# A fused hybrid block on one core: PSUM pools in another order, routing weights as powers of e, row numbers and counts taken later

## The chip, the core and the metric

The kernel runs on one core of one Trainium2 chip. The metric is the device time of one launch in microseconds (us). A core has five engines that run their own instruction streams: TensorE (PE, with its weight loads as PEld), VectorE (DVE), ScalarE (ACT), GpSimd (POOL) and SyncE (SP, which here only issues DMAs). They meet at semaphores. Matmuls write to PSUM, which has eight banks[...].

## The reference

Two layers on an image batch `x` of 2 x 256 x 56 x 56. Layer 0 is a group norm, a 1x1 and a depthwise 3x3 convolution to q, k and v, neighbourhood attention (7x7 windows, one half of the heads with dilation 1, one with dilation 2) and a projection. Layer 1 turns the image into 6272 tokens of 256 channels and does linear attention and a mixture of experts:

```python
t = _to_tokens(x)
t = t + _L1_attn_ref(_ln_t(t), ...)          # linear attention, Q = elu(q)+1, K = elu(k)+1
t = t + _L1_ffn_ref(_ln_t(t), ...)           # 8 experts, the two best of each token
...
logits = xt @ Wr + br
probs = softmax(logits); top_p, top_idx = top_k(probs, 2)
weights = top_p / top_p.sum(axis=-1)         # of two: 1/(1+d) and d/(1+d), d = e^(m1-m0)
xn = layernorm(xt)
h = gelu(xn * ln_g[e] + ln_b[e]) @ W1[e] + b1[e]), y = h @ W2[e] + b2[e]
out = sum of weights * y of the two experts
```

## The kernel before

**Stages.** The convolutions of both images run beside the attention of image 0 (0 to some 420 us). Then the linear attention of the tokens of image 0 (`linear`, half 0) runs beside the rest of the convolutions, to 748 us; then the attention of image 1 (`Attention`, with the bank pool `Banks`) beside the first expert tiles, to some 1050 us; then the linear attention of image 1 (half 1) beside further expert tiles, to 1450 us; then the remaining expert tiles with the output. The 6272 tokens are taken in groups of four blocks of 128 rows (`order`), the last ones in smaller groups.

**Order.** Within `tc.manual_schedule` TensorE's order is the program's. The parts of a group are generators (`queries`, `message`, `feed_forward`, `route`), and strings such as "mqfpPPPPfmqfrfrff" say which one goes a step further: r is the route of the current group, p and P that of the group before it. The other engines' orders are set by a planner when the kernel is built, by priority and estimated readiness; `tc.issue_after(x)` puts an instruction behind x in that order. At run time each engine takes its instructions in its order.

**Routing (`route`).** A group's first step takes the router's logits (`pa`, evacuated to `la`), the token norm, and the normalised rows `row`. The second turns `la` back (L2058), finds the two best experts (`top_two`: maxima `ms`, one-hot `ohs`), adds up the counts per expert before each block (`before`, and the running `cnt`, L2066 to L2069) and computes the two weights of each token (`weights`, L2007: DVE subtracts, ACT does Exp at L2011, DVE the rest) into `row`. The third multiplies with a triangular matrix (L2073, L2074: `pp`) for each token's slot in its expert's list, and casts it to `si`; the stores of the tokens to `y2` are issued from ACT (L1974). Four more steps scatter the rows to `xs` by indirect DMAs from POOL (L2089, helper L167), eight for a full group.

**The seam.** `layer1` leaves the end of the last two groups' routes of half 0 to a generator `ending`, whose five steps are taken inside the attention of image 1, at the step numbers in `ENDING`: the last group but one's `pp`; its scatters and the last group's second step; the counts of full tiles (`full_tiles`: a matmul on `cnt`, L1387, then DVE's table) and the last group's `pp`; its scatters; the rest of the table. From step `LEAD` (22) on, the expert tiles run one step at each attention step: `Experts.fetch` of tile 0 loads `xr` from `xs` once all scatters of these tokens have landed. The attention turns `ld` tiles with TensorE (L759, into `x` banks) and evacuates them to `qT` and `kT` (ACT L768, L771, L777, L784; DVE L779). A chunk is a score matmul `s_ps` (L644), Exp on ACT (L648), a product with a table on DVE (L649), and a value matmul `po` (L658).

**PSUM.** Pools of half 0, in order: `ps_a` two banks, `ps_h` three, `ps_q` two. When they close, the attention opens `po` (two banks), `x` (two), `s_ps` (four), in the same place. `ps_h` holds the feed-forward's results, read last by DVE (L1958); `ps_q` the queries' and the turned messages.

**Expert tiles (`Experts.run`).** For each tile of 256 rows: `fetch` of the next one (from SP: `xr`, L1536, w1e, L1540, w2e, L1544; DVE: `eq`, L1550, L1553, L1554, row numbers `idi`, L1552, and the expert's scale `so`, `sv`), first matmuls `ph` (L1600) with Gelu on ACT (L1604), `turn` of the next tile (TensorE L1569, DVE `xe` L1572, POOL `yt`, L1582), second matmuls `py` (L1618), DVE `yt` (L1624) and a scatter with addition to `y2` (POOL, L167).

Of the kernel before, what the change touches and what calls it, by code (L numbers as in the profile page):

```python
# [13 lines left out]
F32 = mybir.dt.float32  # L14
AF = mybir.ActivationFunctionType
ALU = mybir.AluOpType
# [45 lines left out]
NFS, NHS = 48, 5  # L62
NFI = 14
LEAD = 22
ENDING = (4, 6, 13, 15, 20)
XW = C + 4


# [57 lines left out]
def hybrid_kernel(ctx: ExitStack, tc: tile.TileContext, a: dict, out: bass.AP):  # L126
# [5 lines left out]
    make_identity(nc, ident)  # L132
    mhalf = const.tile([P, 4], F32, name="mhalf")
    nc.vector.memset(mhalf, -0.5)


    td = dram.tile([B * T, C], F32, name="td")
# [461 lines left out]
    class Attention:  # L599
# [116 lines left out]
        def run(self):  # L716
# [126 lines left out]
            def band0(r):  # L843
                yield blocks(8 * r + 16)
                if banks is not None and r == 0:
                    for k in range(2):
                        turning.extend(prepare(k))
                        if k == 0:
                            self.ahead[0, 0] = self.fetch(0, 0)
                    ready[0] = 2  # L850
                yield from prepared(r + 1, 1)
                spare = self.spare if r == 0 else None
                v0 = (spare or vp).tile([TT, 4, P], F32, name="v0", bufs=1 if spare else 2)
                for c in range(4):
                    nc.sync.dma_start(
                        v0[:, c, :],
                        yimg[8 * r : 8 * r + 8, c * KC : (c + 1) * KC, 2 * C : 2 * C + P],
                    )
                if banks is not None and r == 0:
                    self.ahead[0, 1] = self.fetch(0, 1)  # L860
                    self.ahead[1, 0] = self.fetch(1, 0)
                i0, i1 = max(0, 8 * r - 3), min(HH, 8 * r + 11)
                ni = i1 - i0
                sums = [None]

                def chunk(hf, c):
                    j0, j1 = max(0, KC * c - 3), min(WW, KC * c + 17)
                    q = qT0[:, i0:i1, j0:j1]
                    got = []

                    def first():
                        got.append(self.scores(
                            TT, [(kT0[r][:, c].rearrange("p r c -> p (r c)"), q, 0)],
                            self.table(0, (r > 0) + (r == NG - 1), (c > 0) + (c == 3)), j1 - j0,
                        ))

                    def rest():
                        if c == 2 * hf:
                            po = self.ps_o.tile([P, 2, 512], F32, name="po")
                            sums[0] = po[:, :, : ni * 31].rearrange("p k (i j) -> p k i j", j=31)  # L880
                        h0 = (0, 25)[hf]
                        sub = sums[0][:, :, :, j0 - h0 : j1 - h0]
                        self.values(
                            TT, got[0], [(None, q, 0, v0[:, c, :], sub[:, 0], sub[:, 1])], c == 2 * hf
                        )

                    return first, rest

                def done(hf):
                    h0 = (0, 25)[hf]  # L890
                    for j, a0, a1 in ((r, i0, 8 * r + 4), (r + 1, 8 * r + 4, i1)):
                        o = 8 * j - 4
                        accumulate(
                            strip0(j)[:, :, a0 - o : a1 - o, h0 : h0 + 31], sums[0][:, :, a0 - i0 : a1 - i0, :]
                        )
                    if hf == 0:
                        return
                    for j in (r, r + 1) if r == NG - 1 else (r,):
                        a0, a1 = max(0, 8 * j - 4), min(HH, 8 * j + 4)
                        self.normalise(  # L900
                            strips0.pop(j)[:, :, a0 - 8 * j + 4 : a1 - 8 * j + 4, :].rearrange("p k r c -> p k (r c)"),
                            o0[:, a0:a1, :].rearrange("p r c -> p (r c)"), (a1 - a0) * WW,
                        )

                for hf in range(2):
                    for c in (2 * hf, 2 * hf + 1):
                        yield from step(*chunk(hf, c), (lambda hf=hf: done(hf)) if c % 2 else lambda: None)
# [439 lines left out]
    class Experts:  # L1347
# [179 lines left out]
        def fetch(self, t, nh, pools):  # L1527

            run = self.tk.run
            full = nh == 2 and t < NTA  # L1530
            tab, k = (self.tab_h, t) if nh == 1 else (self.tab_a, t) if full else (self.tab_b, t - NTA)
            x = SimpleNamespace(t=t, nh=nh, full=full)
            xr = x.xr = pools.xr()[:, :nh, :]
            e = self.value(tab.tab[0:1, 0, k : k + 1], E - 1)
            r = self.value(tab.tab[0:1, 1, k : k + 1], E * RG + (NDUM - 1) * ST)
            ins = nc.sync.dma_start(xr, xs[bass.ds(r, nh * P), :].rearrange("(p j) c -> p j c", j=nh))  # L1536
            if full:
                apart(ins.ins, [f"xfull{run}"], [f"xlate{run}", f"fill{run}"])
            x.w1 = self.w.tile([P, 2, FF], F32, name="w1e")
            nc.sync.dma_start(  # L1540
                x.w1, a["L1_ffn_W1"][bass.ds(e, 1)].rearrange("one (ct p) f -> p (one ct) f", p=P)
            )
            x.w2 = self.w.tile([P, NJ, C], F32, name="w2e")
            nc.sync.dma_start(  # L1544
                x.w2, a["L1_ffn_W2"][bass.ds(e, 1)].rearrange("one (j p) d -> p (one j) d", p=P)
            )
            x.e = e
            x.eq = self.small.tile([P, 2], F32, name="eq")
            eq = x.eq[:, :nh]
            nc.vector.tensor_scalar(eq, xr[:, :, C + 3], tab.etm[:, k : k + 1], None, ALU.is_equal)  # L1550
            x.idi = self.small.tile([P, 2], mybir.dt.int32, name="idi", bufs=4)
            nc.vector.tensor_copy(x.idi[:, :nh], xr[:, :, C])  # L1552
            nc.vector.tensor_tensor(eq, eq, xr[:, :, C + 2], ALU.mult)  # L1553
            nc.vector.tensor_tensor(eq, eq, xr[:, :, C + 1], ALU.add)  # L1554
            so = self.small.tile([P, 4 + NJ, E], F32, name="so")
            nc.vector.tensor_tensor(
                so, self.sel, tab.oh[:, k, :].unsqueeze(1).to_broadcast([P, 4 + NJ, E]), ALU.mult
            )
            x.sv = self.small.tile([P, 4 + NJ], F32, name="sv")
            nc.vector.tensor_reduce(x.sv, so, AX.X, ALU.add)  # L1560
            return x

        def turn(self, x, pools):
# [7 lines left out]
            for ct in range(2):  # L1571
                newest[0] = nc.vector.tensor_scalar(  # L1572
                    x.xe[:, ct, :], px[:, ct, :nh, :].rearrange("p j t -> p (j t)"),
                    x.sv[:, ct : ct + 1], x.sv[:, 2 + ct : 3 + ct], ALU.mult, ALU.add,
                ).ins
            b2 = pools.b2e()
            nc.sync.dma_start(
                b2, a["L1_ffn_b2"][bass.ds(x.e, 1)].rearrange("one d -> (one d)").partition_broadcast(P)
# [61 lines left out]
    def linear(ph, tk, half, behind=None):  # L1640
# [4 lines left out]
        def pool(name, bufs, **kw):  # L1645
            return ph.enter_context(
                tc.tile_pool(name=f"{name}{run}{half}", bufs=bufs, reuse_waits="tile", **kw)
            )
# [1 line left out]
        bufs = {"e": 1, "s": 3, "t": 1, "q": 1, "w": 1, "k": 2, "l": 2}  # L1650
        pools = {k: pool(f"p3{k}", bufs[k]) for k in ("e t q w k l s", "e s t q k w l")[half].split()}
        kp, sm, tp, wqp, wp, wk, lp = (pools[k] for k in "estqwkl")
        ps_a, ps_h, ps_q = pool("p3pa", 2, space=PSUM), pool("p3ph", 3, space=PSUM), pool("p3pq", 2, space=PSUM)
        ps_k = pool("p3pk", 1, space=PSUM) if half else None
        tk.place(half, tp, lp)

# [324 lines left out]
        def top_two(rt, lg, up, lb, scale, row, n):  # L1981
# [22 lines left out]
                ohs.append(oh)  # L2004
            return ohs, ms

        def weights(rt, ms, row, n):  # L2007

            r = rt.sm.tile([P, 4], F32, name="rsum")[:, :n]
            nc.vector.tensor_tensor(ms[1], ms[1], ms[0], ALU.subtract)  # L2010
            nc.scalar.activation(ms[1], ms[1], AF.Exp)  # L2011
            nc.vector.tensor_scalar(r, ms[1], 1.0, None, ALU.add)
            nc.vector.reciprocal(r, r)
            nc.vector.tensor_tensor(row[:, :n, C + 1], ms[1], r, ALU.mult)
            nc.vector.tensor_scalar(ms[0], ms[1], -1.0, 1.0, ALU.mult, ALU.add)
            nc.vector.tensor_tensor(row[:, :n, C + 2], ms[0], r, ALU.mult)

        def route(n0, n, lb):
# [48 lines left out]
            for k in range(n):  # L2067
                nxt = before[:, k + 1, :] if k < n - 1 else cnt
                nc.vector.tensor_tensor(nxt, before[:, k, :], m[:, k, :], ALU.add)  # L2069
            weights(rt, ms, row, n)  # L2070
            yield
            pp = ns.bank()[:, : 4 * E].rearrange("p (k e) -> p k e", e=E)
            nc.tensor.matmul(pp[:, :n], rt.tri, m[:, :n], start=True, stop=False)  # L2073
# [9 lines left out]
            store(n0, n)  # L2083
            late = [f"xlate{run}"] if (n0, n) in order[early1:] else []
            yield
            for k in range(n):
                with tc.issue_after(newest[1]) if late else nullcontext():
                    for kk in range(K):
# [75 lines left out]
    def layer1(whole, tk, conv_ctx=None, conv=None, behind=None):  # L2164


        run = tk.run
        conv = conv or none

        def fill(n=1):  # L2170
            for _ in range(n):
# [263 lines left out]
```

## Time and profile before

| | us |
|---|---|
| Median of 3 runs | 2003.97 (2000.4 to 2013.45) |
| The profiled execution | 2003.56, of it span from first to last instruction 2001.8 |
| Granted TensorE clock, mean | 0.969 |
| Linear attention, half 0, ends (last `pa`) | 748.2 |
| First L759 of image 1's attention | 751.0 |
| First scores of image 1 | 762.0 |
| First expert matmul (L1600) | 798.0 |
| First matmul of half 1's keys | 1048.8 |
| Last `py` | 1978.4 |

A line of the order of time has: start, duration, engine, line, operation, out<-in, shapes, count, and in brackets the engine's idle time before it and what ended that wait. A line of the waits has: engine, what it waited to do, on what, the sum in us, how often, the longest. Copies of engine names with a q (SPq, ACTq) are sequencers: they wait, branch and issue.

| Operation (before) | engine | number | mean us |
|---|---|---|---|
| Exp of routing weights L2011, 128x4 | ACT | 14, four with a table load of 1.28 | 0.20 |
| power of -1/2, L2043, 128x4 | POOL | 14 | 1.0 |
| power of -1/2, L261, mostly 128x2 | POOL | 90 | 0.70 to 0.80 |
| row scatter to `xs`, L167 | POOL | 98 | 1.03 |
| row numbers L1552 | DVE | 53 | 0.18 |

### The profile page before, as it was taken

The page shows a single profiled execution, that of the slowest core. Times are in us where ns is not written, and L with a number is a line of the kernel's source. Part 1 is how long each engine was busy: PE and PEld are TensorE (multiplying, and loading weights), DVE is VectorE, ACT ScalarE, POOL GpSimd, SP SyncE. Part 2 cuts the span into 40 slices and gives each one's busy share as a digit, 9 for nine tenths or more (in the row PEclk, how much of TensorE's full clock was granted, in tenths as well). Part 3 has the DMA queues.
Part 4 walks back from the last instruction along what each step waited for, and adds up shares of the span by engine and source line. Part 5 has one row for each costly group of instructions (what it writes and reads, how often), then busy time and mean ns, then how long its engine had stood idle before and what let it go on. Part 6 is the DMA issues. An engine that isn't in the chain of part 4 may idle for free.

```text
span 2001.8 us, 27731 instructions
## 1 busy us (share of the span) xinstructions
PE 1842.0 (92%) x9996; PEld 1308.3 (65%) x9996; DVE 1094.2 (55%) x2733; ACT 704.5 (35%) x1331; POOL 582.2 (29%) x634
## 2 busy tenths in 40 slices
PE   6999898988889996899989989999899999999996
PEld 3545354556555654566668756567688888888885
DVE  6978988888887746555557434554531212121221
ACT  2333324324434323445536433323322232323332
POOL 4630221025102444111126311445422222222221
PEclk9999999989999996999999999999999999999998
DMA  4753432340001534654474211114577676766995
GB/s 112 160 138 110 133 92 75 111 146 17 25 38 42 157 85 145 193 152 134 129 201 127 56 34 37 48 57 132 156 230 200 188 199 189 198 190 195 299 279 161
DMA packets 200153, 268.85 MB, mean 134 GB/s; under 512 B 30953, under 2 KB 158615, under 8 KB 199761
## 3 DMA queue, kind: packets, MB, share of 16 engines
q1 hardware_dynamic: 167920, 223.95, 37.0%
q0 software_dynamic: 19728, 27.54, 7.5%
q10 hardware_dynamic: 12352, 15.43, 2.2%
q8 instruction: 83, 1.36, 0.3%
q14 instruction: 70, 0.57, 0.1%
HBM read 200.19 MB, written 70.95 MB: 135 GB/s over the span
## 4 chain that ended last, share of the span: by engine, by line
PE 47%; DMA 4%; DVE 4%; ACT 3%; issue 1%; POOL 1%; SPq 0%; ACTq 0%; DVEq 0%; POOLq 0%
PE ph L1600 13%; PE py L1618 13%; PE p L1935 4%; PE x L1618 2%; DMA y<-yt,idi 2%; PE x L1600 2%; PE py L1951 2%; PE po L658 2%; DMA xr<-xs 1%; PE kx L309 1%; PE kp L297 1%; PE x L349 1%; PE pm L1905 1%; PE s_ps L644 1%; PE px L1569 1%
## 5 line engine op out<-in xcount | busy, mean ns | idle before, releaser
L1600 PE MATMUL ph<-xe,w1e 128*128 128x256 f32 (+1 forms) x1448 | 312.1, 371 | 15.3 <-ACT hT L1604 9.4
L1618 PE MATMUL py<-w2e,hT 128*128 128x256 f32 x1392 | 311.5, 379 | 0.0
L1604 ACT ACTIVATE hT<-ph,sv 128x256 f32<-128x256 f32 (+1 forms) x362 | 165.7, 462 | 393.4 <-PE ph L1600 386.1
L1600 PEld LDWEIGHTS ph<-xe,w1e 128*128 128x128 f32 x1448 | 262.6, 191 | 55.0 <-ACT hT L1604 11.2
L1618 PEld LDWEIGHTS py<-w2e,hT 128*128 128x128 f32 x1392 | 260.2, 190 | 33.2 <-issue 0.2
L167 POOL DMA_INDIRECT y<-yt,idi x101 | 160.2, 1587 | 325.4 <-DVE yt L1624 186.9
L571 DVE SCALAR_TENSOR_TENSOR yc<-ypad,w,yc 128x1120 f32<-128x1120 f32 x144 | 202.8, 1412 | 26.4 <-ACT yc L561 18.5
L261 POOL TENSOR_TENSOR rs<-rs,mhalf 128x2 f32<-128x2 f32 (+3 forms) x90 | 72.1, 805 | 323.6 <-DVE rs L260 292.7
L521 PE MATMUL py<-x_sb,wq 128*128 128x448 f32 (+1 forms) x384 | 153.8, 532 | 5.4 <-ACT ypad L527 3.8
L648 ACT ACTIVATE p<-s_ps 112x952 f32<-112x952 f32 (+5 forms) x88 | 102.1, 1160 | 154.6 <-PE s_ps L644 96.0
L1552 DVE CAST idi<-xr 128x2 int32<-128x2 f32 (+1 forms) x53 | 9.8, 184 | 258.6 <-DMA xr<-xs 258.4
L649 DVE TENSOR_TENSOR p<-p,tab 112x952 f32<-112x952 f32 (+5 forms) x88 | 122.0, 1389 | 45.5 <-ACT p L648 39.6
L542 PE MATMUL pc<-ypad,diag 128*128 128x448 f32 x324 | 131.9, 548 | 0.0
L1624 DVE SCALAR_TENSOR_TENSOR yt<-py,eq,yt 128x256 f32<-128x256 f32 x87 | 41.8, 482 | 156.6 <-PE py L1618 156.4
L1582 POOL TENSOR_SCALAR yt<-b2e,eq 128x256 f32<-128x256 f32 x101 | 50.4, 505 | 251.5 <-DMA b2e<-in_L_ffn_b 209.0
L167 POOL DMA_INDIRECT xs<-row,si x98 | 100.5, 1026 | 71.9 <-DVE si L2082 41.9
L521 PEld LDWEIGHTS py<-x_sb,wq 128*128 128x128 f32 x384 | 71.7, 197 | 67.1 <-issue 56.8
L564 DVE SCALAR_TENSOR_TENSOR yc<-ypad,w,yc 128x784 f32<-128x784 f32 x96 | 101.8, 1077 | 4.2 <-ACT yc L561 3.6
L658 PE MATMUL po<-p,v 98*32 98x170 f32 (+5 forms) x960 | 71.2, 379 | 29.1 <-issue 12.6
L542 PEld LDWEIGHTS pc<-ypad,diag 128*128 128x128 f32 x324 | 59.8, 191 | 52.4 <-issue 48.7
L1935 PE MATMUL p<-m2T,fw 128*128 128x512 f32 (+2 forms) x224 | 93.8, 542 | 0.0
L1935 PE MATMUL p<-xT,fw 128*128 128x512 f32 (+1 forms) x208 | 92.7, 568 | 0.0
(391 smaller groups left out, 2891.1 us busy)
## 6 DMA issues: line engine op xcount, KB each, us to landing
w1e<-in_L_ffn_W SPq DMA_DIRECT2D x53, 1024.0 KB
w2e<-in_L_ffn_W SPq DMA_DIRECT2D x53, 1024.0 KB
yd<-yc SPq DMA_DIRECT2D x24, 784.0 KB
ld<-yd SPq DMA_DIRECT2D x28, 448.0 KB
xr<-xs SPq DMA_DIRECT2D x48, 260.0 KB
b2e<-in_L_ffn_b SPq DMA_DIRECT2D x53, 128.0 KB
t<-td SPq DMA_DIRECT2D x12, 512.0 KB
y<-t ACTq DMA_DIRECT2D x24, 256.0 KB
```

Of the source, the lines that this page charges most:

```text
L167: ins = nc.gpsimd.indirect_dma_start(out=dst[:, :], out_offset=bass.IndirectOffsetOnAxis(ap=index, axis=0), in_=src, in_offset=None, **kw,)
L521: nc.tensor.matmul(py[:, :n, :], self.wq1[:, ct, oc * P : (oc + 1) * P], self.x_sb[:, ct, (q0 + g0) * WW : (q0 + g0 + n) * WW], start=(ct ...
L542: nc.tensor.matmul(pc, diag[:, tap, :], ypad[:, dy : dy + SHARE, dx : dx + WW], start=(tap == 0), stop=(tap == 8),)
L564: nc.vector.scalar_tensor_tensor(yc[:, y0:y1, :], src, w, yc[:, y0:y1, :], ALU.mult, ALU.add)
L571: nc.vector.scalar_tensor_tensor(yc[:, y0:y1, :], src, w, yc[:, y0:y1, :], ALU.mult, ALU.add)
L648: nc.scalar.activation(p[:nk, :, :n], s_ps[:nk, :, :n], AF.Exp)
L649: nc.vector.tensor_tensor(grid(p), grid(p), table[:nk], ALU.mult)
L658: nc.tensor.matmul(dst[hs] if w is None else den[hs], v[:nk, hs] if w is None else w[:nk, :], p[:, h, :, o : o + q.shape[2]], start=first ...
L1600: nc.tensor.matmul(p1, x.w1[:, ct, j * P : (j + 1) * P], x.xe[:, ct, :], start=(ct == 0), stop=(ct == 1),)
L1604: nc.scalar.activation(hT[:, j, :], p1, AF.Gelu, bias=x.sv[:, 4 + j : 5 + j])
L1618: nc.tensor.matmul(py, hT[:, j, h * P : (h + 1) * P], x.w2[:, j, :], start=(j == 0), stop=(j == NJ - 1),)
L1935: nc.tensor.matmul(p1[:, :w], fw1[:, k, oc * P : (oc + 1) * P], rhs, start=(k == 0), stop=(k == 3))
```

## The change

1. In half 0, `ps_q` is opened before `ps_h`, so the attention's `x` banks lie where `ps_q` was.
2. `weights` is split. `power` does the subtraction and then, on POOL and behind the newest scatter, a power with base e (`euler`, a constant tile); it stays in the route's second step. The rest of `weights` moves to the step of the first scatter.
3. `eq` and `idi` move from `fetch` to `turn`, after `xe`.
4. `ENDING` takes the counts and the last group's `pp` three steps later (16 for 13), its scatters two steps later (17 for 15).
5. In the attention of image 1, for bands after the first, the loads of `v0` are issued before `prepared`, which issues the loads of `ld`.

```diff
-ENDING = (4, 6, 13, 15, 20)
+ENDING = (4, 6, 16, 17, 20)
...
+    euler = const.tile([P, 4], F32, name="euler")
+    nc.vector.memset(euler, float(np.e))
...
+                spare = self.spare if r == 0 else None
+
+                def values():
+                    v0 = (spare or vp).tile([TT, 4, P], F32, name="v0", bufs=1 if spare else 2)
+                    for c in range(4):
+                        nc.sync.dma_start(
+                            v0[:, c, :],
+                            yimg[8 * r : 8 * r + 8, c * KC : (c + 1) * KC, 2 * C : 2 * C + P],
+                        )
+                    return v0
+
+                ahead = banks is not None and r > 0
+                v0 = values() if ahead else None
                 yield from prepared(r + 1, 1)
-                spare = self.spare if r == 0 else None
-                v0 = (spare or vp).tile([TT, 4, P], F32, name="v0", bufs=1 if spare else 2)
-                for c in range(4):
...
+                v0 = v0 or values()
...
-            x.eq = self.small.tile([P, 2], F32, name="eq")
-            eq = x.eq[:, :nh]
-            nc.vector.tensor_scalar(eq, xr[:, :, C + 3], tab.etm[:, k : k + 1], None, ALU.is_equal)
-            x.idi = self.small.tile([P, 2], mybir.dt.int32, name="idi", bufs=4)
-            nc.vector.tensor_copy(x.idi[:, :nh], xr[:, :, C])
-            nc.vector.tensor_tensor(eq, eq, xr[:, :, C + 2], ALU.mult)
-            nc.vector.tensor_tensor(eq, eq, xr[:, :, C + 1], ALU.add)
+            x.etm = tab.etm[:, k : k + 1]
...
+            x.eq = self.small.tile([P, 2], F32, name="eq")
+            eq, xr = x.eq[:, :nh], x.xr
+            nc.vector.tensor_scalar(eq, xr[:, :, C + 3], x.etm, None, ALU.is_equal)
+            x.idi = self.small.tile([P, 2], mybir.dt.int32, name="idi", bufs=4)
+            nc.vector.tensor_copy(x.idi[:, :nh], xr[:, :, C])
+            nc.vector.tensor_tensor(eq, eq, xr[:, :, C + 2], ALU.mult)
+            nc.vector.tensor_tensor(eq, eq, xr[:, :, C + 1], ALU.add)
...
-        ps_a, ps_h, ps_q = pool("p3pa", 2, space=PSUM), pool("p3ph", 3, space=PSUM), pool("p3pq", 2, space=PSUM)
+        ps_a = pool("p3pa", 2, space=PSUM)
+        if half:
+            ps_h, ps_q = pool("p3ph", 3, space=PSUM), pool("p3pq", 2, space=PSUM)
+        else:
+            ps_q, ps_h = pool("p3pq", 2, space=PSUM), pool("p3ph", 3, space=PSUM)
...
+        def power(ms):
+
+            nc.vector.tensor_tensor(ms[1], ms[1], ms[0], ALU.subtract)
+            with tc.issue_after(newest[2]) if newest[2] else nullcontext():
+                nc.gpsimd.tensor_tensor(ms[1], euler[:, : ms[1].shape[1]], ms[1], ALU.pow)
+
         def weights(rt, ms, row, n):
 
             r = rt.sm.tile([P, 4], F32, name="rsum")[:, :n]
-            nc.vector.tensor_tensor(ms[1], ms[1], ms[0], ALU.subtract)
-            nc.scalar.activation(ms[1], ms[1], AF.Exp)
...
-            weights(rt, ms, row, n)
+            power(ms)
             yield
...
             yield
+            weights(rt, ms, row, n)
             for k in range(n):
...
+        newest[2] = None
```

More of the change, by code (lines that the diff above doesn't have):

```diff
@@ L850, in band0 @@
                     ready[0] = 2
-                yield from prepared(r + 1, 1)
-                spare = self.spare if r == 0 else None
-                v0 = (spare or vp).tile([TT, 4, P], F32, name="v0", bufs=1 if spare else 2)
-                for c in range(4):
[L855 to L858, printed above, removed]
+                spare = self.spare if r == 0 else None
[9 more added lines that the diff above has]
+                v0 = values() if ahead else None
+                yield from prepared(r + 1, 1)
+                v0 = v0 or values()
                 if banks is not None and r == 0:
```

## The prediction

> **What bounds the kernel now.** I read the page first (busy shares, slices, granted clock), then busy time by stretch, TensorE's waits around the seam, then the order of time of each engine where a wait is long.
>
> ```profile
> PE 1842.0 (92%) x9996; PEld 1308.3 (65%) x9996; DVE 1094.2 (55%) x2733; ACT 704.5 (35%) x1331; POOL 582.2 (29%) x634
> ...
> PE   6999898988889996899989989999899999999996
> ...
> PEclk9999999989999996999999999999999999999998
> ```
>
> TensorE is the bound at 92%. Slice 16 (750 to 800 us) is the seam where the linear attention's first half hands over to the second image's attention: busy 6, clock 6. Time taken from a TensorE wait there should reach the end: from 1452 to 1865 us TensorE has no gap over 0.15 us, and the tail (last `py`, its scatter, the read back, the output) starts from TensorE's last tile.
>
> ```profile
> 748.00:800.00 52.00, 33.50 (x259) 20.56 (x252) 35.17 (x158) 16.49 (x37) 21.72 (x23) 0.70 0.45 139
> 832.00:842.00 10.00, 5.33 (x36) 2.96 (x37) 5.90 (x13) 2.73 (x5) 0.93 (x2) 0.66 0.38 92
> 1400.00:1412.00 12.00, 6.18 (x30) 5.38 (x29) 5.24 (x34) 4.53 (x8) 3.61 (x5) 0.72 0.40 120
> ```
>
> Columns: stretch, length, then busy us of TensorE, its weight loads, DVE, ACT, POOL, then clock. The seam has 18.5 us without TensorE and a clock of 0.70; the two others are single gaps that the change also touches. Its gaps from 745 to 1050 us, the single long ones (total, times, longest):
>
> ```profile
> PE po L658 <- remote: 4.9, 1, 4.9
> PE x L1387 <- DVE cnt L2069: 4.7, 1, 4.7
> PE po L658 <- issue: 4.7, 1, 4.7
> PE x L759 <- issue: 2.8, 1, 2.8
> ...
> PE x L759 <- ACT qT L768: 2.2, 1, 2.2
> PE x L1600 <- DVE xe L1572: 1.7, 1, 1.7
> ```
>
> The 4.7 put down to "issue" is no issue: at 837.2 `po` waits for `p` of DVE, and DVE stands in its queue behind a row-number cast that waits for `xr` to land:
>
> ```profile
> 837.20 1.02 PE L658 MATMUL po<-p,v 112*32 112x238 f32 x8 [4.67 <-issue]
> ```
>
> ```profile
> 835.17 0.17 DVE L1552 CAST idi<-xr 128x2 int32<-128x2 f32 x1 [7.94 <-DMA xr<-xs]
> ...
> 835.96 1.14 DVE L649 TENSOR_TENSOR p<-p,tab 112x952 f32<-112x952 f32 x1
> ```
>
> The third gap, at 1407.7: the Exp of the routing weights stands in ACT's queue, loads its table, waits 4.58 us for DVE's `m`, and the Gelus that TensorE needs are behind it:
>
> ```profile
> 1399.83 1.28 ACT L2011 ACT_TABLE_LOAD   x1
> 1405.69 0.20 ACT L2011 ACTIVATE m<-m 128x2 f32<-128x2 f32 x1 [4.58 <-DVE m L2010]
> 1405.91 1.28 ACT L1604 ACT_TABLE_LOAD   x1
> ```
>
> ```profile
> 1407.73 2.08 PE L1600 MATMUL ph<-xe,w1e 128*128 128x256 f32 x4 [5.82 <-ACT hT L1604]
> ```
>
> **What the Trainium skill says.** (1) *PSUM — Partial Sum Buffer*, "Engine vs sequencer instructions": the queues of ScalarE, VectorE and GpSimdE are strict FIFO. The last two fences agree: a waiting cast and a waiting Exp hold up ready work. (2) *TensorE: Matmul & The Clock Gate*, Part 1 (the clock gate): TensorE drops to half clock after an idle window of about 3.4 us. The trace agrees: its clock records fall to 0.5 at 752.8, 773.3, 786.9, 834.7 and 1404.8 us, each with one of these gaps. (3) *ScalarE: Activation LUTs*, "What ACT_TABLE_LOAD costs": 1283 ns; the trace has 1.28 us, and 4 of the 14 Exps carry one.
>
> **The change part by part.**
>
> *PSUM order.* `x` moves from two banks of `ps_h` to the two of `ps_q`. The 2.84 us gap before the first L759 (751.01) ends as DVE's last L1958 leaves a `ps_h` bank (750.91); `ps_q` is free long before, so 8 transposes can start at 748.2. Next late is the group's `pp` (L2073, 755.84): it needs `before`, which DVE finishes at 755.76. So the 2.84 and the 2.24 behind it mostly turn into that wait. Gained there: five weight operations leave DVE's queue ahead of `before` (0.16 us each, 0.08 apart: 0.4 us). After it the waits for evacuations (0.83, 0.48) go. Sum 1.7 us; from both sides 0 to 5.1.
>
> *Powers instead of Exp.* In the seam ACT waits 4.24 us at the Exp (753.52), but a store of `t` at 752.86 waits beside it: 0.3 us, counted above. At 1407.7 the 5.82 us go, with the half clock until 1411.6 (3.9 us of work at half speed: 1.9). Next late: `before` of that group, DVE 1406.8; TensorE would arrive at L2073 at 1401.9 + 0.8 + 4.3 = 1407.0 instead of 1413.6, so 6.6 us. Cost: 14 powers on POOL, by the same operation and shape (L2043) 1.0 us each, 14 us on an engine 29% busy, each put behind the newest scatter and waiting for `m`. Behind it stand the 90 `rs` powers (L261, 0.70 us), for which ACT, DVE and then TensorE wait. From both sides: 0, to 14 + the 21.5 us that ACT waited at L2011 = 35.5. I take 1.5, since POOL sits idle 2 to 4 us before most L261 already.
>
> *Row numbers at the turn.* The four operations (0.16 to 0.23 us) no longer wait for `xr` in the fetch. At 837.2: `p` comes after ACT's L648 (833.2) plus 1.14, so TensorE resumes at 834.4, 2.8 us earlier, and the half clock after it (4.35 us, half lost) may go: 2.1. At 1048.8 (gap 1.22) and 1431.05 (1.25) the same cast delays DVE: 1 us of each two. Sum 6. Added: four operations after `xe`, before POOL's `yt`, which `py` needs some 7 us later: 0, covered by L1618.
>
> *Counts three steps later.* The 4.73 us before L1387 go. But DVE, ACT and SP all wait until 772.2 for TensorE's own transposes, recorded at 767.3: the trace does not show whether the values could run meanwhile. And the last group's `pp` now stands behind values, scores, values (774.56 to 779.54: 4.4 us of work). What hangs on it:
>
> ```profile
> 786.64 2.43 DMA xs<-row,si
> 789.09 2.67 DMA xr<-xs
> ```
>
> From `pp` (773.6) `si` is 3.6 us, eight scatters 10.2, landing 2.4 behind the last issue: 15.5 to 789.1. Then w1e lands at 795.5 (6.4), while `xe` came at 798.0 because DVE did chunks first. Best case: `pp` at 773.6 − 1.7 − 4.4 + 4.4 = 771.9, first L1600 at 771.9 + 21.9 = 793.8 instead of 798.0. If the stall to 772.2 stays: 770.5 + 4.4 = 774.9, so 796.8. I take 795 (gain 3, the 1.7 above included), bounds +2 to −14 (the 18.4 less some 4 that the scatters need). The 4.87 at 789.9 is of the same unexplained kind, and TensorE then waits for `xr`.
>
> *v0 ahead of ld.* Four DMAs (0.66 to 0.71 us of SP each) pass two `ld` (0.32, 0.39) in six bands; `ld` is issued 2.8 us later, with its transposes two steps or more off, but v0 no longer stands behind an `ld` that waited 12.7 us. 0, from −1 to +1. *`euler`*: one memset in the first stage, 0.
>
> Sum: −3 (seam) −6.6 −6 +1.5 = −14. The profiled execution took 2003.56 us (span 2001.8), 0.4 below the median of 2003.97; −14 gives **1990**.
>
> **Rivals.** *The scatters become the seam's bound* (27%): `pp` late, seam +2, POOL 3: −12.6 + 5 = −8, 1996. For: 15.5 us from `pp` to landing. Against: the DVE wait behind `xr` also goes. *The seam closes* (18%): the stalls at 772 and 789 go with the waits: 14 there, 25 in all, 1979. For: gaps plus half clock hold 28. Against: DVE is busy 35 of 52 us there. *POOL in the way* (7%): the powers wait for `m` ahead of L261 in POOL's queue, in all 14 groups; 35.5 − 12.6 = +23, 2027. It decides once POOL's added waits exceed 12.6 us in total. For: ACT's waits at the same place were 21.5. Against: L261 goes out at high priority. *It does nothing* (6%): other waits fill each gap, 2004. The forecast has 42%.
>
> **How the numbers follow.** 1% (20 us) is about what a measurement of this kernel can tell from no change. Faster by more: most of the closing seam and the edge of the forecast, 0.20. Slower: POOL, 0.07. Within: 0.73. The range 1977 to 2007 takes in three cases and the +2/−14 of the seam; POOL and the far edge of the closing seam stay out.
>
> **What would show it.** L2011 gone from ACT, its 4 loads gone, no gap over 2 us near 1407; DVE with no wait on `xr` at 801, 813, 835, TensorE's gap there near 1.9; L759 at 748 and a new wait at L2073; first L1600 near 795 of its own time. It is wrong if L261 waits grow on POOL, if TensorE waits over 8 us for `xr` before the first tile, or if the tail does not move up with the tiles.

## The result, and the profile after

| | before | changed |
|---|---|---|
| Median of 22 runs each, us | 2005.97 | 2012.03 |
| Ratio, 95% interval | | 1.0029 [1.0017, 1.0040] |
| Profiled execution, span | 2001.8 | 2009.6 |
| Last `pa` of half 0 to first expert matmul | 49.9 | 57.2 |

The kernel became about 6 us slower, where 14 us less was forecast. The page of the changed kernel answers the first fence of the forecast; TensorE's work is the same and the seam's slice has fallen from clock 6 to 5:

```profile
PE 1846.9 (92%) x9996; PEld 1310.7 (65%) x9996; DVE 1091.0 (54%) x2734; ACT 692.1 (34%) x1309; POOL 597.6 (30%) x648
...
PE   6999898988899996999989989999899999999996
...
PEclk9999999989999995999999999999899999999998
```

**Where the time went.** TensorE has the same matmuls in both kernels, nearly all in the same order, so the n-th matmul of a kind in one trace can be set against the n-th in the other. The lag of the changed kernel, that is how much later it runs the same matmul, in the two profiled executions:

| Around (us of before) | lag | step there |
|---|---|---|
| 740 | +0.5 | |
| 825 | +9.0 | seam, +8.5 |
| 855 | +3.4 | the wait at 837 is gone, −5.6 |
| 1403 | +1.4 | small ones, −2.0 |
| 1430 | −2.9 | the wait at 1407 is shorter, −4.3 |
| 1460 | +4.7 | new wait, +7.5 |
| 1550 | +9.1 | new wait, +4.4 |
| 1975 | +7.8 | −1.3 |

So two of the forecast's gains are there, and three losses are larger than they. Busy time by stretch, with the columns of the forecast's second fence; the last stretch is new:

```profile
748.00:800.00 52.00, 28.97 (x211) 17.77 (x211) 30.58 (x154) 13.28 (x31) 23.94 (x25) 0.60 0.35 108
832.00:842.00 10.00, 9.73 (x117) 6.69 (x117) 5.06 (x10) 8.03 (x10) 1.60 (x1) 1.00 0.73 180
1400.00:1412.00 12.00, 10.31 (x55) 8.87 (x54) 6.58 (x43) 3.02 (x7) 5.55 (x8) 0.91 0.72 224
1440.00:1452.00 12.00, 6.86 (x26) 5.68 (x25) 5.51 (x42) 1.90 (x4) 7.49 (x10) 0.81 0.49 146
```

The two single gaps are filled; the seam has lost 4.5 us more of TensorE. Its waits from 745 to 1050 us are no longer for the counts but for attention's product `p` and for `qT`:

```profile
PE po L660 <- DVE p L651: 11.4, 3, 7.3
...
PE x L761 <- ACT qT L770: 5.9, 1, 5.9
```

DVE in order of time has two long waits in the seam. The first is 5.88 us at the first weight operation (L2030), which needs the power from POOL. The program has the weight operations in a later step now, but in DVE's order they still stand ahead of `chosen` (L2082), from which the counts and `pp` are made:

```profile
773.33 0.17 DVE L2030 TENSOR_SCALAR rsum<-m 128x4 f32<-128x4 f32 x1 [5.88 <-POOL m L2025]
...
773.66 0.16 DVE L2082 TENSOR_TENSOR chosen<-oh,oh 128x32 f32<-128x32 f32 x1
...
797.98 0.23 DVE L1581 TENSOR_SCALAR eq<-xr,etmA 128x2 f32<-128x2 f32 x1 [7.96 <-DMA xr<-xs]
```

POOL shows why the power was late: it stands last behind the eight scatters of the group before, whose spacing is 1.27 us.

```profile
770.00 0.96 POOL L169 DMA_INDIRECT xs<-row,si  x1 [0.30 <-issue]
771.26 0.96 POOL L169 DMA_INDIRECT xs<-row,si  x1 [0.30 <-issue]
772.24 1.05 POOL L2025 TENSOR_TENSOR m<-euler,m 128x4 f32<-128x4 f32 x1
```

The second DVE wait (7.96 us for `xr`) goes with late scatters: `pp` of the last group ran 7.1 us later, and so did the first expert matmul (805.2 for 798.0). TensorE, before and changed:

```profile
773.59 0.61 PE L2073 MATMUL x<-chosen,tri 128*128 128x32 f32 x2
```

```profile
780.72 0.61 PE L2091 MATMUL x<-chosen,tri 128*128 128x32 f32 x2
```

At 1447 the power of the last, small group comes after four scatters of its predecessor; DVE, in order of time, waits with `rsum`, and `chosen` is behind it again. POOL first, then DVE, then TensorE:

```profile
1443.58 0.96 POOL L169 DMA_INDIRECT xs<-row,si  x1 [0.30 <-issue]
1444.84 0.96 POOL L169 DMA_INDIRECT xs<-row,si  x1 [0.30 <-issue]
1445.82 0.59 POOL L2025 TENSOR_TENSOR m<-euler,m 128x1 f32<-128x1 f32 x1
```

```profile
1441.73 0.15 DVE L2023 TENSOR_TENSOR m<-m,m 128x1 f32<-128x1 f32 x1
...
1446.44 0.15 DVE L2030 TENSOR_SCALAR rsum<-m 128x1 f32<-128x1 f32 x1 [4.43 <-issue]
...
1446.95 0.40 DVE L2082 TENSOR_TENSOR chosen<-oh,oh 128x8 f32<-128x8 f32 x1
```

```profile
1447.40 0.59 PE L2091 MATMUL pp<-chosen,tri 128*128 128x8 f32 x2 [4.88 <-DVE chosen L2082]
```

"issue" beside DVE's 4.43 us is again no issue: it ends with the power. The subtraction was done at 1441.9, and the power of 0.59 us could not start for 3.9 us. In the section "Engine vs sequencer instructions" of *PSUM — Partial Sum Buffer* the Trainium skill says that the queues of ScalarE, VectorE and GpSimdE are strict FIFO (first in, first out); here it holds twice in a row, on POOL and then on DVE.

At 1407 the same happens on a small scale. The lag fell by 7.4 us there at first, and 3.1 of them were lost again within some 10 us: DVE waited 0.68 us for the power, the weight operations and then `chosen` came after it, and TensorE waited before `pp`:

```profile
1408.97 0.37 PE L2091 MATMUL pp<-chosen,tri 128*128 128x16 f32 x2 [1.69 <-DVE row L2034]
```

The loss near 1508 is of another kind. DVE's cast of row numbers waits 9.07 us for an `xr`, and `xe`, whose `px` was turned at 1498.6 already, is behind it:

```profile
1507.69 0.17 DVE L1583 CAST idi<-xr 128x2 int32<-128x2 f32 x1 [9.07 <-DMA xr<-xs]
...
1507.93 0.99 DVE L1575 TENSOR_SCALAR xe<-px,sv 128x256 f32<-128x256 f32 x2
```

The cast belongs to the tile after the one whose `xe` it delays; it was to be at the turn, but in DVE's order it is not. The whole run's row for it says that next to nothing was gained. Before and changed:

```profile
L1552 DVE CAST idi<-xr 128x2 int32<-128x2 f32 (+1 forms) x53 | 9.8, 184 | 258.6 <-DMA xr<-xs 258.4
```

```profile
L1583 DVE CAST idi<-xr 128x2 int32<-128x2 f32 (+1 forms) x53 | 11.5, 216 | 250.2 <-DMA xr<-xs 248.6
```

### The profile page after: what moved, and what is told of

It reads as the page before. It is cut to its first block, busy times and chain, and to the rows that moved or that the text cites. A ratio compares the mean times of both kernels' runs of the same rounds, so it can differ in the third digit from the quotient of the medians.

```text
span 2009.6 us, 27727 instructions
## 1 busy us (share of the span) xinstructions
PE 1846.9 (92%) x9996; PEld 1310.7 (65%) x9996; DVE 1091.0 (54%) x2734; ACT 692.1 (34%) x1309; POOL 597.6 (30%) x648
## 4 chain that ended last, share of the span: by engine, by line
PE 45%; DMA 6%; DVE 4%; ACT 3%; issue 1%; POOL 1%; SPq 0%; DVEq 0%; ACTq 0%; POOLq 0%
PE ph L1610 12%; PE py L1628 12%; PE p L1949 4%; PE x L1628 2%; DMA y<-yt,idi 2%; PE x L1610 2%; DMA xs<-in_c_fill 2%; PE po L660 2%; PE py L1965 1%; DMA xr<-xs 1%; PE x L351 1%; PE kx L311 1%; PE kp L299 1%; PE pm L1919 1%; PE px L1572 1%
## 5 line engine op out<-in xcount | busy, mean ns | idle before, releaser
L263 POOL TENSOR_TENSOR rs<-rs,mhalf 128x2 f32<-128x2 f32 (+3 forms) x90 | 71.3, 796 | 282.2 <-DVE rs L262 240.7
```

## The experiments

Five theories: A, DVE's queue stands at the power; B, POOL itself is late whatever DVE does; C, the later steps of the ending make the seam late; D, the loads of `v0`, not the row numbers, took the wait at 837; E, the row numbers have to be held to move at all. (Experiment 10 has a sixth, F.) The seam's length is again from the last `pa` of half 0 to the first expert matmul. Ratios are to the kernel before, run in turn with each. Beside the first eight runs the kernel before took 2005 to 2006 us; beside the last four it took 1996.08.

**1. Weights behind the cast to `si`.** Changed kernel, with:

```diff
-            weights(rt, ms, row, n)
+            with tc.issue_after(cast.ins):        # cast: the last copy to si
+                weights(rt, ms, row, n)
```

> Changed kernel, but the remaining weight operations (L2030 and on) stand behind the cast to si in DVE's order; POOL's order and everything else as in the changed kernel. Theory A (DVE's queue: the first weight operation waits for the power, which stands behind the previous group's row scatters on POOL, and holds the count chain behind it): the 4.88 us gap before the last group's pp near 1447 goes with its half clock (7.5), the 2.43 us gap near 1508 goes with its half clock (4.4), DVE's wait of 5.9 us for the power near 767 goes; span 2009.6 - 12 - 1 to 4 = 1994 to 1997. Theory B (POOL's queue: the power and the scatters themselves are too late, whatever DVE does first): the gaps stay, within 2 us of 2009.6. Theory C (the seam's new order of steps is the whole loss): 1447 and 1508 change, the seam stays at +8.5 against the kernel before.

Ratio 0.9995 [0.9980, 1.0010] instead of 1.0029: some 7 us gained, about half of what was expected. The last group's `pp` in TensorE's order of time has no wait; the gap near 1508 is gone too:

```profile
1449.01 2.86 PE L1610 MATMUL ph<-xe,w1e 128*128 128x256 f32 x12 [0.40 <-DVE xe L1575]
1451.91 0.39 PE L2091 MATMUL pp<-chosen,tri 128*128 128x8 f32 x2
```

A holds for 1447, and B falls: POOL's order is the same. At 1407 the lag now falls by 7.2 us where the changed kernel kept 4.3. But the seam is as long as before the mend (56.6 us), so DVE's wait at the power was not what set it. The profiled execution took 4.4 us more than this kernel's median, so its span of 2007.3 is not compared.

**2. The ending's old steps.** Changed kernel, with:

```diff
-ENDING = (4, 6, 16, 17, 20)
+ENDING = (4, 6, 13, 15, 20)
```

> Changed kernel with the steps of the ending at 4, 6, 13, 15, 20 as before. Theory C (the later steps delay pp of the last group, its eight scatters and so the first expert tile): pp near 776 instead of 780.7, the wait of DVE for xr (7.96 us at 798) shrinks by some 4.7, span 2004 to 2006. Theory A: the DVE wait for the power near 767 stays at some 5.9 us and the count comes after 775, so pp not before 775.7; the gaps at 1447 and 1508 stay. If the steps' place is not what costs: span within 1.5 us of 2009.6.

Ratio 1.0014 [0.9999, 1.0029]. `pp` ran 28.2 us after the last `pa` instead of 32.9, and the seam took 52.3 us instead of 57.2: 4.9 us, as C had it. The gap at 1447 stays (4.68 us), while the one near 1508 is gone, against the expectation. The seam is read from one trace of each kernel; the intervals of the two ratios overlap, so the times alone don't show the gain.

**3. Both.** 

> Both edits: weights behind the cast to si, and the ending at 4, 6, 13, 15, 20. Theories A and C together: pp of the last group at 770 to 774, xr landed by 790, first expert matmul by 796, no gap over 2 us at 1447 or 1508; span 1988 to 1993, ratio to the kernel before 0.993 to 0.995. If the seam's loss is neither (unexplained late completions of TensorE): the seam stays within 2 us of the kernel before (first expert matmul near 798) and the span is 1994 to 1998.

Ratio 0.9978 [0.9965, 0.9992]: faster than before, by 4 to 5 us rather than the 10 to 14 expected. `pp` came 27.1 us after `pa`, but its scatters started 6.2 us after it (3.6 before), since they now wait for the weights too, so the seam took 54.8. And the gap of `xe` behind the cast is back, 3.21 us at 1495.

**4. Row numbers at the turn, alone.** Kernel before, with part 3 of the change.

> Kernel before with the row numbers and eq at the turn alone. The step of the forecast: the 4.67 us gap at 837.2 falls to some 1.9, its half clock goes, 4.9 there; about 1 us together at 1049 and 1431; nothing at the seam or at 1407. Span 2001.8 - 5 to 6 = 1996 to 1997, ratio 0.997 to 0.9975. Rival: eq at the turn puts a wait for xr ahead of attention's products in DVE's order at the first tile, as in the changed kernel (7.96 us at 798): then the gap before po there grows and the gain is under 2 us.

Ratio 0.9993 [0.9974, 1.0012]. DVE in order of time still casts first, and the product waits behind it:

```profile
838.77 0.21 DVE L1574 CAST idi<-xr 128x2 int32<-128x2 f32 x1 [8.96 <-DMA xr<-xs]
...
839.60 1.14 DVE L649 TENSOR_TENSOR p<-p,tab 112x952 f32<-112x952 f32 x1
```

TensorE's gap there is 5.73 us. The forecast's step did not happen: the program's order changed, and the planner put the cast where it had been, ahead of six attention products.

**5. `v0` ahead of `ld`, alone.** Kernel before, with part 5.

> Kernel before with the loads of v0 ahead of those of ld alone; eq and idi stay in the fetch. Theory D (the order of the loads, through the planner's estimates, moves the row-number cast of one tile in DVE's order from ahead of six attention products to just ahead of that tile's xe): the 4.67 us gap at 837 goes to under 0.5 with its half clock, 5 to 5.5 us gained there, though no row-number line is touched; span 2001.8 - 5.3 = 1996 to 1997.5, ratio 0.997 to 0.9975. Forecast (v0 costs and gains nothing, the row numbers do): gap stays at 4 to 6 us, within 1 us of 2001.8 but for the scatter of single executions.

Ratio 0.9975 [0.9960, 0.9989]. No row-number line was touched, and TensorE's gap is gone. DVE's order now has the products first and no cast in this stretch; TensorE, then DVE:

```profile
831.97 0.61 PE L658 MATMUL po<-p,v 112*32 112x238 f32 x8 [0.27 <-PE x L759]
```

```profile
830.00 0.81 DVE L832 TENSOR_TENSOR acc<-po,acc 128x224 f32<-128x224 f32 x2 [3.61 <-PE po L658]
830.72 1.14 DVE L649 TENSOR_TENSOR p<-p,tab 112x952 f32<-112x952 f32 x1
```

D holds: in the order of DVE's instructions in the built kernel, this cast went from ahead of six products to just ahead of its tile's `xe` (two others moved by three or four places). In the rest of the run DVE waited as long for `xr` as ever (244 us).

**6. Exp on ACT again.** Changed kernel, with the powers undone.

> Changed kernel with the powers undone: Exp on ACT and all weight operations in the route's second step. Theory A: the gaps at 1447 (4.9) and 1508 (2.4) are absent, the 5.8 us gap near 1407 is back with its half clock, DVE does not wait near 767; net of 1400 to 1550: 3.7 against the 7.7 lost by the changed kernel, that is 4 us less. The last group's pp at 776 to 781 by the later steps, so the first expert tile stays late (wait for xr of 5 to 8 us at the seam). Span 2003 to 2006. If instead the power is what makes the seam late, the first expert matmul is by 799 and the span is 1998 to 2001.

Ratio 0.9995 [0.9981, 1.0008]. 1447 and 1508 are without gap, 1407 has its 5.83 us back, and the seam still takes 55.6 us. DVE has no power to wait for there, and waits for `xr` all the same:

```profile
795.90 0.23 DVE L1581 TENSOR_SCALAR eq<-xr,etmA 128x2 f32<-128x2 f32 x1 [7.96 <-DMA xr<-xs]
```

Its profiled span, 1999.3, is under the 2003 to 2006 expected, with the seam as late as expected and the rest of the run earlier. So the powers don't set the seam; with them the changed kernel lost more at 1447 and 1508 than it gained at 1407.

**7. Row numbers held behind `xe`.** Kernel before, with part 3 and:

```diff
+            with tc.issue_after(newest[0]):       # newest[0]: the second xe
                 nc.vector.tensor_scalar(eq, xr[:, :, C + 3], x.etm, None, ALU.is_equal)
                 nc.vector.tensor_copy(x.idi[:, :nh], xr[:, :, C])
```

> Kernel before with the row numbers and eq at the turn, and this time held behind xe in DVE's order. Theory E (the move in the program alone left DVE's order as it was; only a hold changes it): DVE waits for xr under 10 us in the whole run where it was 258, the 4.67 us gap at 837 goes (5.3), the 1.2 us gaps at 1049 and 1431 shrink by 1 each; span 1994.5 to 1996.5, ratio 0.9965 to 0.9975. Rival: xe itself, which needs the turned xr, is placed where the cast was and waits as long: gap at 837 within 1 us of 4.7, ratio 0.999 to 1.

Ratio 0.9966 [0.9949, 0.9983]. The cast's row for the whole run has no wait left, where it had 258 us:

```profile
L1575 DVE CAST idi<-xr 128x2 int32<-128x2 f32 (+1 forms) x53 | 8.5, 160 | 0.0
```

The lag fell by 5.6 us at 837 and by 0.9 at 1431, near the forecast's 4.9 and 1. The rival, that `xe` waits in its place, falls.

**8. Three mends on the changed kernel** (1, 2 and 7). 

> Changed kernel with three mends: weights behind the cast to si, the ending at 4, 6, 13, 15, 20, row numbers held behind xe. Against the kernel with the first two mends (ratio 0.9978): the 5.5 us gap before po at the first tile, where DVE waited 7.0 us for xr, goes or halves, and the 3.2 us gap near 1495 goes with its half clock; 5 to 9 us less, ratio 0.9935 to 0.9955. If xr's landing itself is the bound there: ratio 0.9965 to 0.998.

Ratio 0.9948 [0.9929, 0.9967]. No gap over 1 us is left from 1365 to 1560.

**9. The ending's later steps alone.** 

> Kernel before with the ending's steps at 4, 6, 16, 17, 20 alone. Theory C (the later steps are the seam's loss: pp of the last group later by the 4.4 us of work it now stands behind, its scatters and the landing of xr with it): pp at 778 to 781, xr lands near 796 to 798, first expert matmul at 803 to 805 instead of 798.0, the 837 gap as before; ratio 1.002 to 1.003. Rival (in the kernel before TensorE waited 4.7 us at that place anyway, so the steps move for nothing): first expert matmul within 1.5 us of 798 after taking off what the run was late by at 740.

Ratio 1.0007 [0.9993, 1.0021]: not to be told from no change by the time. In the last four runs the wait of 4.7 us before the counts is not there to be saved (1.3 us or less in the three kernels with the old steps), and `pp` ran 23.3 us after `pa`, against 19.2 to 22.5 in those three. TensorE waited 7.80 us at the first tile, behind this:

```profile
784.34 0.23 DVE L1550 TENSOR_SCALAR eq<-xr,etmA 128x2 f32<-128x2 f32 x1 [8.06 <-DMA xr<-xs]
```

The wait is no mark of the later steps: experiments 10 and 11 have the old ones, and TensorE waits 7.35 and 7.19 us at this place. By the letter the rival's number is met: the run was 3.2 us early at 740 and the first expert matmul came at 791.5, 6.5 before 798.0. But that compares with a trace that had the wait. Among the last four runs the seam took 47.7 us here and 44.7 to 48.2 in the three with the old steps, so this run doesn't decide for C. For C stand the traces of the two kernels and the first eight runs: 55.6 to 57.2 us in the three with the later steps, 49.9 to 54.8 in the seven with the old ones.

**10. The PSUM order alone.** 

> Kernel before with the PSUM pools of half 0 reordered alone. Forecast step: the 2.84 us gap before the first L759 goes, a wait takes its place behind the first eight transposes, 1.7 us gained by the group's pp, bounds 0 to 5.1. Theory F (ACT's queue decides: the evacuation to qT stands behind the store and the Exp, both due near 753.5, so eight transposes that start 2.8 us earlier only wait behind themselves): gap of 5 to 6 us after eight transposes, 0 to 0.5 us gained; first scores at 762 to the half us after taking off what the run was late by at 740; ratio 0.999 to 1.0005.

Ratio 0.9999 [0.9985, 1.0013]. The transposes start at once, and then wait 3.76 us; in the kernel of experiment 9, also of the last four and with the old order, the two gaps sum to 1.48 + 2.24 = 3.72. The first scores come 12.5 us after the last `pa` in both.

```profile
743.04 0.99 PE L759 MATMUL x<-ident,ld 112*128 112x112 f32 x8
747.79 1.74 PE L759 MATMUL x<-ident,ld 112*128 112x112 f32 x8 [3.76 <-ACT qT L768]
```

ACT in order of time has the reason: `qT` stands behind the store of `t` and the Exp.

```profile
746.44 0.37 ACTq L1978 DMA_DIRECT2D y<-t  x1
747.10 0.20 ACT L2015 ACTIVATE m<-m 128x4 f32<-128x4 f32 x1 [3.99 <-DVE m L2014]
747.21 0.53 ACT L768 ACTIVATE qT<-x 128x448 f32<-128x448 f32 x1
```

In the changed kernel, without the Exp, it waits for the store alone: `qT` at 754.26, the store at 753.80, gap 5.95. F holds, though the wait is shorter than its 5 to 6 us; the gain is 0.

**11. The powers alone, weights behind the cast to `si`.** 

> Kernel before with the powers alone and with the weight operations held behind the cast to si. Theory A: the 5.82 us gap at 1407 goes with its half clock (7 to 8 us, as in the changed kernel), no gap over 3 us near 1447 or 1508, the seam within 1.5 us of the kernel before; ratio 0.996 to 0.997. Rival (POOL's 14 powers late everywhere): under 4 us.

Ratio 1.0000 [0.9986, 1.0013], a miss. At 1407 the lag falls by 7.2 us, as expected, and is given back: 2.8 at 1421 and 3.6 at 1496. Both times the row-number cast waits in DVE's queue, ahead of the evacuation that releases ACT, or of `xe`; DVE, then TensorE:

```profile
1417.98 0.17 DVE L1554 CAST idi<-xr 128x2 int32<-128x2 f32 x1 [7.16 <-DMA xr<-xs]
...
1494.60 0.45 DVE L1554 CAST idi<-xr 128x2 int32<-128x2 f32 x1 [8.85 <-DMA xr<-xs]
```

```profile
1420.60 1.13 PE L1602 MATMUL ph<-xe,w1e 128*128 128x256 f32 x4 [2.35 <-ACT hT L1606]
...
1495.70 4.60 PE L1602 MATMUL ph<-xe,w1e 128*128 128x256 f32 x20 [3.35 <-DVE xe L1574]
```

TensorE comes earlier, `xr` does not, and the cast hands the difference on.

**12. Powers and held row numbers.** Kernel before, with the edits of 7 and 11. 

> Kernel before with the powers, the weight operations behind the cast to si, and the row numbers held behind xe; PSUM order, ending and v0 as before. If the two gains add: rows held (ratio 0.9966, 7 us) and powers (7 us): ratio 0.992 to 0.994, and not slower than the three mends on the changed kernel (0.9948). If the seam gives back part, as it did there (first expert matmul 3 us late against 740): ratio 0.995 to 0.996.

Ratio 0.9934 [0.9916, 0.9952], 1983.21 us: faster than both kernels, and the lowest ratio of all runs, though its interval overlaps that of experiment 8. The gain at 1407 (7.2 us) now stays to the end, and none of the gaps of experiment 11 is left. So the two gains do add, as expected: 7 us at 1407 and 5.6 at 837. PSUM order, ending and `v0` are those of before. It has 5 timed runs.

## Why the prediction was wrong

**PSUM order, −1.7:** wrong, 0. The prediction named the store of `t` beside the Exp and counted 0.3 us for it; it is the store that the evacuation, and so the next eight transposes, wait for. With TensorE earlier the wait is longer by as much (3.76 us for 1.48 + 2.24 in experiment 10).

**Powers, −6.6, POOL +1.5:** the gain was sized well for a kernel whose DVE does not stand at the power (7.2 in experiments 1, 11, 12). The step that failed here is the cost, which put DVE's queue at nothing: "each put behind the newest scatter and waiting for `m`. Behind it stand the 90 `rs` powers". It asked who waits behind the power on POOL, and not what stands ahead of it, though 1.27 us for each of up to eight scatters was in the working, nor who waits for its result: DVE, with the counts behind. It even took for granted that "five weight operations leave DVE's queue ahead of `before`"; four had stood there, and in the changed kernel they stand ahead of `chosen` at 773, 1408 and 1446, with the power to wait for. L263's waits did not grow (282 us in all, 324 before). Undoing the hold at DVE brought the ratio from 1.0029 to 0.9995, some 7 us for the 1.5 that were charged. The loss near 1508 is the cast's: it is gone for good where the row numbers are held (experiments 8 and 12), while among the kernels that don't hold them it comes and goes (absent in 1, 2 and 6; a wait of 3.2 and 3.4 us in 3 and 11).

**Row numbers, −6:** the sum was nearly right at 837 (5.6 for 4.9) and its cause was wrong: "no longer wait for `xr` in the fetch". Moving the lines left DVE's order as it was (experiment 4); **`v0` ahead**, costed at 0, moved the cast (experiment 5). Bounds of −1 to +1 came from SP's time alone; that a planner orders DVE anew was not in them.

**Counts three steps later, −1.3 net:** wrong in sign. The prediction worked out that 4.4 us of work would stand ahead of `pp`, and set 4.4 us of saved waiting against them; in the trace `pp` came 7.1 us later, and the first tile 7.1 us later. The first rival of the prediction, scatters as the seam's bound, comes nearest to what happened, at 8.5 us for its 2. From experiment 2, 4.9 us of the seam's 7.3 are the steps' place, close to the 4.4 us of work; the saving against them was taken up by other waits (3.79 and 1.18 us for attention's `p`). The remaining 2.4 are about what traces of such kernels differ by: experiments 4, 5 and 7 leave parts 1, 2 and 4 of the change out, and their seams took 51.7 to 52.0 us, beside 49.9 before and 52.3 in experiment 2.

**The sum:** −3 −6.6 −6 +1.5 was forecast; +8.5, −4.3, −7.6 and +11.9 (1447 and 1508) were found in the pair of traces, with +0.5 before the seam and −1.3 after. The rival for the other side had POOL as its engine, but with the `rs` powers waiting in all 14 groups. Those didn't wait longer; it was DVE that waited for the routing power, in 12 of the 14 groups for 0.7 to 5.9 us, and TensorE waited behind it at 1447 and for 1.7 us at 1409. Of the signs that were named for a wrong forecast, neither longer waits at `rs` nor a wait of TensorE over 8 us for `xr` (it was 7.3) came.

**Clock:** the prediction set the falls to half clock beside an idle window of about 3.4 us. Shorter gaps were enough: before, the clock also fell at 1060.0 and 1363.8 us, with single gaps of 1.96 and 2.01 us, and in the changed kernel at 1409.8, with the gap of 1.69. So a gap of 2 us can already cost more than itself.

**Open:** before 772 us in the kernel before, ACT, DVE and SP wait for TensorE's transposes recorded until 767.9. Experiment 10 has the same transposes followed by their evacuation within 0.1 us. None of the last four runs has it, though they hold the old steps and the new. The wait ends 2.5 us after the start of the last of a group's eight scatters, and the wait of DVE that ends at 788.8 in the same way 2.2 us after that of the next group (786.64):

```profile
769.75 0.96 POOL L167 DMA_INDIRECT xs<-row,si  x1 [0.30 <-issue]
```

```profile
772.22 0.25 ACT L182 COPY kT<-x 128x112 f32<-128x112 f32 x1 [3.85 <-remote]
```

Experiments 2, 4, 5 and 7 have both waits too, each ending 2.2 to 2.6 us after such a scatter. But the last four runs have the same scatters without the waits, so that the scatters cause them isn't shown; what it is was not found.

## What to carry to other kernels

When an operation moves to another engine, price both queues: what stands ahead of it there, and what stands behind the first instruction that needs its result. Where a planner orders an engine, moving lines moves nothing by itself, while an edit elsewhere can; compare the engine's order before and after, and hold the instruction if it has to be late. A gain on the bound engine lasts only while the next arrival is early enough: mend the wait that would take it back (here the cast) in the same change.

## What was not expected of the hardware

The kernel before took 2005 to 2006 us beside the first eight runs and 1996.08 beside the last four; in the traces of those four the transposes' completions before the counts were seen some 4 us earlier against their records. Whether the one explains the other isn't shown.

A load of `xr` (260 KB) landed 2.7 us after its issue at the seam of the kernel before (789.09). In the changed kernel the load issued at 1494.08 landed after 2.8 us, and the next one, issued at 1497.22 behind two weight loads of 1024 KB (1494.94 and 1495.52), after 10.35 us.
